# A two-layer graph network on one core: four more tiles' step 0 output made between the parts of step 1's first list, and the tail's tiles in another order

## Chip, cores and metric

One core of a Trainium2 chip runs the whole program in one launch. The metric is device time in microseconds (us), from the first to the last instruction and what lies around it. Lower is better. The engines are PE (matrix products and transposes; PEld is its weight load), ACT (pointwise functions and copies out of the accumulators), DVE (vector operations, maxima, sums), POOL (simple vector operations and indirect DMAs) and SP (which only issues DMAs). Each takes its instructions strictly in order.

## The reference, cut to what matters

`x` has 3327 rows of 256 numbers, `adj` is a sparse 0/1 matrix of 3327 x 3327. Layer 0 is a graph attention with a gated update, and its result, normalized by row, is `X` for layer 1:

```python
R = S + eye(N); R = R / R.sum(-1, keepdims=True)      # S is adj
Z = 0; Xf = X; Xa = X
for n in range(2):                                     # "step 0" and "step 1"
    A  = top_p_attention(Xa, W1, W2, W3)               # softmax, keep the largest to 0.9 of the sum
    Xf = R @ Xf
    Xa = A @ Xa
    Z  = Z + Xf @ U1[n].T + Xa @ U2[n].T
h = X + Z
out = layernorm(h) * ln_g + ln_b
x = layernorm(X + out)
```

The output of a row needs four products with 256 x 256 matrices: two of step 0 (`Xf @ U1[0].T`, `Xa @ U2[0].T`) and two of step 1.

## The kernel before

Rows are cut into 26 tiles of 128 (the last has 127). Step 0 of layer 1 handles one tile every 32 turns of a hand-written order. Step 1 handles the tiles one after another in a pipelined loop: while PE transposes and multiplies the attention of tile i (`product`), DVE sorts the logits of tile i+1 (`list_1`, `list_2`, `list_3`) and masks them (`mask`), and ACT takes exponentials (`exp`, `exp_list`). Rows whose list was too short are put aside, and up to three tiles of them ("hard" tiles) are worked off in the tail.

Three stages matter here.

**The gap between step 0 and step 1.** Tile 0 of step 1 has no product before it, so its list is made alone: `list_1(NT)`, two `exp`, `list_2`, `exp_list`, `list_3`, `mask`, `put_aside_1`, and only then the loop with `propagate` (a product with the adjacency) and `product`. The order of PE, ACT and DVE in this block is the order of the text (`manual_schedule`). POOL and SP are placed by the framework's scheduler, which also hands out the buffers.

**The early ends.** For the first `HALVES` = 10 tiles the two step 0 products are made during the last tiles of step 0 (`early_ends`). A tile's five parts are `transposes` (four transposes of its rows `xfe` and of `xa`), `copy` (ACT, accumulator to `xt`), `load_next` (the load of the tile two further on), `terms` (eight matmuls and the addition of `X` as a product with the identity, into `pze`) and `store` (ACT copies `pze` to `z`, SP writes it to `z0_rows` in DRAM). The rows `xfe` come from DRAM into a buffer of the tag `xf`, of which there are two. The loop's own rows (`xf`, made by `fetch`) have the same tag, and the tiles `z` share the tag `own`, also of two, with a tile that `propagate` fills on POOL.

**The tail.** `ends` works off the hard tiles on DVE (`bound`, `hard`), each followed by a product on PE (`hard_end`), and opens one `tile_end` after another between them: 0.8 for each turn. A tile end loads its rows, transposes them, multiplies, and normalizes twice over ACT, DVE and POOL. In this text an F tile is one whose end makes both steps (16 of them: two loads of rows and one of `X`, eight transposes, 16 matmul instructions plus two for `X`) and an H tile one whose step 0 part is read back from `z0_rows` (10 of them: half the transposes and half the matmuls). The order before is all F tiles (10 to 25), then all H tiles (0 to 9).

Of the kernel before, what the change touches and what calls it, by code (L numbers as in the profile page):

```python
# [9 lines left out]
F32 = mybir.dt.float32  # L10
# [6 lines left out]
P = 128  # L17
N = 3327
D = 256
DC = D // P  # L20
DA = 64
NT = (N + P - 1) // P
# [65 lines left out]
]  # L88
AT_0 = {name: tick for tick, name in ORDER_0}

HALVES = 10

GROUP = (208, 167)
LIST = (40, 72)
# [14 lines left out]
def rows(t):  # L109
    return TAIL if t == NT - 1 else P  # L110
# [13 lines left out]
def move_rows(engine, dst, src, r):  # L124

    full = r // 16 * 16
    for a, b in ((0, full), (full, r)):
        if a < b:
            engine.dma_start(dst[a:b], src[a:b])
# [170 lines left out]
class SlowLayer1:  # L300
# [33 lines left out]
    def transposed(self, srcs, r, tag):  # L334

        nc = self.nc
        xt = self.work.tile([P, 2 * DC, P], F32, tag="xt", name=f"xt{tag}")
        pt = self.psm.tile([P, 2 * DC, P], F32, tag="sm", name=f"ptx{tag}")
        for s, a in enumerate(srcs):
            for c in range(DC):  # L340
                nc.tensor.transpose(pt[:, s * DC + c, :r], a[:, c * P : (c + 1) * P], self.ident[:r, :r])
        m = len(srcs) * DC
        nc.scalar.copy(xt[:, :m, :r], pt[:, :m, :r])
        return xt
# [827 lines left out]
class Layer1:  # L1172
# [52 lines left out]
    def setup_0(self, keep, dram):  # L1225

        nc, sh = self.nc, self.sh


        self.fromend = keep.tile([P, 1], F32, name="fromend")  # L1230
        nc.vector.tensor_scalar(self.fromend, sh.rowid[:, 0:1], -1.0, float(P), ALU.mult, ALU.add)
        self.block = keep.tile([P, NT], BF16, name="block")
        nc.vector.tensor_scalar(self.block, sh.col1[:, :NT], -1.0, float(NT), ALU.mult, ALU.add)

        self.places_l = keep.tile([P, UL], BF16, name="places_l")
        nc.vector.tensor_scalar(self.places_l, sh.col1[:, :UL], -1.0, None, ALU.add)
        self.places_h = keep.tile([P, UH], BF16, name="places_h")
        nc.vector.tensor_scalar(self.places_h, sh.col1[:, :UH], -129.0, None, ALU.add)
        self.zeros = keep.tile([P, NT], F32, name="zeros26")
        nc.vector.memset(self.zeros, 0.0)  # L1240

        self.needed = keep.tile([P, NT], F32, name="needed")
        self.ulist = dram.tile([NT, UB * P], F32, name="ulist")

        self.z0_rows = dram.tile([HALVES * P, D], F32, name="z0_rows")

    def sparse(self, t):

# [350 lines left out]
    def early_ends(self):  # L1599


        nc, sh = self.nc, self.sh
        while self.phase <= EVERY0 * (NT - 1) + AT_0["logits3"]:
            yield
        self.load_u1()
        xfs, xts, pzs = {}, {}, {}

        def load(t):
            xfs[t] = self.work.tile([P, D], F32, tag="xf", name=f"xfe{t}")
            move_rows(nc.sync, xfs[t][: rows(t)], sh.xf_rows[t * P : t * P + rows(t), :], rows(t))  # L1610

        def load_next(t):
            if t + 2 < HALVES:
                load(t + 2)

        def transposes(t):
            turn = self.transposing((xfs.pop(t)[: rows(t)], self.xa[: rows(t), t, :]), rows(t), f"et{t}")
            next(turn)
            xts[t] = turn

        def copy(t):
            xts[t] = next(xts[t])

        def terms(t):
            pzs[t] = self.pac.tile([P, 512], F32, tag="av", name=f"pze{t}")
            self.output_terms(pzs[t], xts.pop(t), 0, (0, 1), rows(t), True, False)
            self.plus(pzs[t], sh.x1[: rows(t), t, :], rows(t))

        def store(t):
            z = self.work.tile([P, D], F32, tag="own", name=f"z0_{t}")  # L1630
            nc.scalar.copy(z[: rows(t)], pzs.pop(t)[: rows(t), :D])
            move_rows(nc.sync, self.z0_rows[t * P : t * P + rows(t), :], z[: rows(t)], rows(t))

        load(0)
        load(1)
        at = {}
        for i, turns in enumerate(((2, 3, 4, 24, 28), (17, 18, 19, 25, 29))):
            at.update(zip(turns, [(i, f) for f in (transposes, load_next, copy, terms, store)]))
        while self.phase % EVERY0 != 5:
            yield  # L1640
        for t in range(0, HALVES, 2):
            for k in range(EVERY0):
                if k in at:
                    i, f = at[k]
                    f(t + i)
                yield

    def first_1(self):


        while self.phase <= EVERY0 * (NT - 1) + max(AT_0[k] for k in ("sign0", "sign1", "xf")):
            yield
        v = self.item(NT)
        self.item(NT + 1)
        self.fetch(NT)
        v.cand = self.candidates(v.r, GROUP[1], v.tag)
        ready, waiting = [], list(range(-(-N // GROUP[1])))
        for pair in self.chunks():
            while self.done * P < min(NT * P, HALF + pair[0][1] + LC):
                yield  # L1660
            for i in (NT, NT + 1):
                self.some_logits(i, pair)
                yield
            ready += [c for h, s in pair for c in range(h * HALF + s, min(N, h * HALF + s + LC))]
            have = set(ready)
            for g in list(waiting):
                if have.issuperset(range(g * GROUP[1], min(N, (g + 1) * GROUP[1]))):
                    waiting.remove(g)
                    self.eights(v.cand, v.l, v.r, GROUP[1], g * GROUP[1], min(N, (g + 1) * GROUP[1]))
            yield  # L1670

    def transposed(self, srcs, r, tag, kind="xt"):

# [284 lines left out]
    def tile_end(self, t, j):  # L1958

        nc, r, sh = self.nc, rows(t), self.sh  # L1960
        on = slice(t * P, t * P + r)
        a = self.work.tile([P, EB, P], F32, tag="m", name=f"xfs{t}").rearrange("p b c -> p (b c)")
        xa2 = self.work.tile([P, D], F32, tag="xf", name=f"xa2_{t}")
        x1 = self.work.tile([P, D], F32, tag="xf2", name=f"x1_{t}")[:r]

        spare = lambda k: sh.qT[:r, k * D : (k + 1) * D]
        h, xb = spare(j % 9), spare(9 + j % 3)
        steps = (0, 1) if t >= HALVES else (1,)
        if 0 in steps:
            move_rows(nc.sync, a[:r, :D], sh.xf_rows[on, :], r)  # L1970
        move_rows(nc.sync, a[:r, D : 2 * D], sh.xf2_rows[on, :], r)
        move_rows(nc.sync, xa2[:r], sh.xa2_rows[on, :], r)
        move_rows(nc.sync, x1, (sh.x1_rows if 0 in steps else self.z0_rows)[on, :], r)
        yield
        srcs = ((a[:r, :D], self.xa[:r, t, :]), (a[:r, D : 2 * D], xa2[:r]))
        xts = [self.transposed(srcs[n], r, f"{'uv'[n]}t{t}") for n in steps]
        yield
        pz = self.pac.tile([P, 512], F32, tag="av", name=f"pzt{t}")
        for n, xt in zip(steps, xts):
            self.output_terms(pz, xt, n, (0, 1), r, n == steps[0], False)  # L1980
        self.plus(pz, x1, r)
        yield
        rest = self.output_rows(pz, [xb], h, r, f"t{t}")
        for k, _ in enumerate(rest):
            if k == 2:
                move_rows(nc.sync, xb, sh.xb_rows[on, :], r)
            yield
        move_rows(nc.sync, self.out[on, :], h, r)
# [255 lines left out]
    def ends(self, bounds):  # L2244


        ends = [self.tile_end(t, j) for j, t in enumerate((*range(HALVES, NT), *range(HALVES)))]
        open_ends, queue = [], []
        ticks = 0

# [49 lines left out]
    def run(self):  # L2300
# [4 lines left out]
            self.step_0()  # L2305
        with self.tc.manual_schedule(engines=engines):
            self.list_1(NT)
            self.exp(NT, 0)
            self.exp(NT, 1)
            self.list_2(NT)  # L2310
            self.exp_list(NT)
            self.list_3(NT)
            self.mask(NT)
            self.put_aside_1(NT)
            for i in range(NT, total):
                if i + 2 < total:
# [141 lines left out]
```

## Time and profile before

| What | Value |
|---|---|
| time, three runs | 1824.83, 1835.53, 1836.32 us (median 1835.53) |
| the profiled execution's own time | 1836.04 us |
| its span, first to last instruction | 1834.2 us |
| mean granted PE clock | 0.927 |
| layer 0 and step 0 | to about 972 us |
| the gap (list of step 1's first tile, alone) | 972 to 988.8 us |
| step 1's loop | 988.8 to about 1577 us, 22.8 us per tile on average |
| the tail | about 1577 to 1834 us |
| last matmul, last store of a tile end | 1798.5 us, 1819.8 us |

The profiled execution agrees with the median of the runs to 0.5 us, so sums can be made against it. Times in the views are us from the start of the span. In a timeline each line gives start, busy time, engine, source line, operation, what it writes and reads, how many were merged, and in brackets the idle time before it and what ended that.

### The profile page before, as it was taken

The page shows a single profiled execution, that of the slowest core. Times are in us where ns is not written, and L with a number is a line of the kernel's source. Part 1 is how long each engine was busy: PE and PEld are TensorE (multiplying, and loading weights), DVE is VectorE, ACT ScalarE, POOL GpSimd, SP SyncE. Part 2 cuts the span into 40 slices and gives each one's busy share as a digit, 9 for nine tenths or more (in the row PEclk, how much of TensorE's full clock was granted, in tenths as well). Part 3 has the DMA queues.
Part 4 walks back from the last instruction along what each step waited for, and adds up shares of the span by engine and source line. Part 5 has one row for each costly group of instructions (what it writes and reads, how often), then busy time and mean ns, then how long its engine had stood idle before and what let it go on. Part 6 is the DMA issues. An engine that isn't in the chain of part 4 may idle for free. (4 is left out here: it accounts for less than half of the span.)

```text
span 1834.2 us, 28832 instructions
## 1 busy us (share of the span) xinstructions
PE 1566.7 (85%) x8445; PEld 1093.6 (60%) x8445; DVE 1398.3 (76%) x4759; ACT 1060.3 (58%) x2398; POOL 1076.7 (59%) x1774
## 2 busy tenths in 40 slices
PE   6489999976898888888788999999999989788972
PEld 4255555544555555555565777777777656577861
DVE  5788887447887887877617999999999877967761
ACT  3366666645667667767624555555555446567544
POOL 1577777634665565555444556666666573655754
PEclk9799999987989898989988999999999999899986
DMA  8877773322333333333331111111111120223231
GB/s 268 293 258 238 232 224 100 83 68 76 94 100 101 87 98 103 91 96 102 92 96 44 47 50 50 53 53 49 47 50 50 49 59 20 67 63 95 78 87 46
DMA packets 115301, 181.38 MB, mean 99 GB/s; under 512 B 27900, under 2 KB 84213, under 8 KB 115136
## 3 DMA queue, kind: packets, MB, share of 16 engines
q0 software_dynamic: 26624, 74.64, 15.6%
q1 hardware_dynamic: 70258, 87.96, 14.9%
q10 hardware_dynamic: 18254, 16.86, 2.8%
q8 instruction: 69, 1.13, 0.2%
q14 instruction: 96, 0.79, 0.1%
HBM read 146.08 MB, written 33.41 MB: 98 GB/s over the span
## 5 line engine op out<-in xcount | busy, mean ns | idle before, releaser
L1917 PE MATMUL pav<-xa,at 128*128 128x256 f32 (+2 forms) x1352 | 331.4, 390 | 7.0 <-ACT at L1903 7.0
L1917 PEld LDWEIGHTS pav<-xa,at 128*128 128x128 f32 (+2 forms) x1352 | 245.7, 191 | 86.7 <-ACT at L1903 38.9
L1716 DVE MAX8 cand<-array 128x8 f32<-128x167 f32 (+5 forms) x921 | 241.3, 336 | 31.4 <-ACT array L1703 23.0
L1703 ACT COPY array<-pl 128x416 f32<-128x416 f32 (+3 forms) x402 | 183.5, 509 | 127.5 <-PE pl L1700 112.4
L1700 PE MATMUL pl<-kT,qT 64*128 64x416 f32 (+3 forms) x804 | 228.4, 599 | 17.3 <-issue 5.6
L647 POOL DMA_INDIRECT g<-xf_rows,edge x130 | 135.8, 1044 | 167.3 <-PE pxf L1860 126.0
L647 POOL DMA_INDIRECT g<-x_rows,edge x130 | 135.5, 1042 | 82.2 <-issue 32.9
L1903 ACT COPY at<-pt 128x512 f32<-128x512 f32 (+2 forms) x182 | 96.3, 542 | 140.7 <-PE pt L1901 95.2
L647 POOL DMA_INDIRECT g<-whx,edge x130 | 141.1, 1085 | 46.4 <-issue 36.1
L1493 POOL DMA_INDIRECT g<-x1k,uidx x130 | 137.4, 1057 | 40.0 <-issue 38.6
L1734 DVE MAX8 lst<-cand 128x8 f32<-128x160 f32 (+3 forms) x364 | 113.5, 312 | 8.1
L1700 PEld LDWEIGHTS pl<-kT,qT 64*128 64x128 f32 (+1 forms) x804 | 77.2, 197 | 68.0 <-issue 33.9
L864 DVE FIND_INDEX8 at<-ones,array 128x8 uint32<-128x840 f32 (+1 forms) x104 | 105.5, 1027 | 0.0
L1832 DVE MATCH_REPLACE8 array<-gone,array 128x3335 f32<-128x3335 f32 (+1 forms) x26 | 94.0, 3617 | 0.0
L1736 DVE MATCH_REPLACE8 cand<-lst,cand 128x160 f32<-128x160 f32 (+3 forms) x312 | 92.9, 298 | 0.0
L1852 POOL TENSOR_SCALAR m<-col,erow 128x128 f32<-128x128 f32 x130 | 76.7, 603 | 1.0
L1860 PE MATMUL pxf<-g,m 128*128 128x256 f32 (+1 forms) x260 | 68.3, 413 | 3.4 <-DVE base L2023 3.4
L985 PE MATMUL acc<-g,m 128*128 128x259 f32 (+1 forms) x260 | 64.8, 397 | 6.8 <-ACT m L981 6.8
L1860 PEld LDWEIGHTS pxf<-g,m 128*128 128x128 f32 (+1 forms) x260 | 50.6, 203 | 31.0 <-issue 20.2
L1488 POOL TENSOR_SCALAR uidx<-back 128x5 uint32<-128x5 f32 x26 | 9.8, 378 | 97.9 <-DMA back<-ulist 97.8
L1554 PE MATMUL pav<-g,w 128*128 128x257 f32 (+1 forms) x260 | 63.7, 389 | 1.2 <-issue 0.7
L1554 PEld LDWEIGHTS pav<-g,w 128*128 128x128 f32 (+1 forms) x260 | 47.1, 189 | 21.6 <-issue 7.0
(568 smaller groups left out, 3897.9 us busy)
## 6 DMA issues: line engine op xcount, KB each, us to landing
array<-in_adj_dram SPq DMA_DIRECT2D x23, 1248.0 KB
array<-in_adj_dram SPq DMA_DIRECT2D x23, 415.5 KB
xf_rows<-xf SPq DMA_DIRECT2D x50, 128.0 KB
xa_rows<-xa SPq DMA_DIRECT2D x50, 128.0 KB
xfs<-xf_rows SPq DMA_DIRECT2D x40, 128.0 KB
whx<-table ACTq DMA_DIRECT2D x25, 129.5 KB
x_rows<-x ACTq DMA_DIRECT2D x25, 128.0 KB
x1k<-x ACTq DMA_DIRECT2D x25, 128.0 KB
```

Source lines behind the costliest of these rows:

```text
L647: self.nc.gpsimd.indirect_dma_start(out=dst[:, b, :], out_offset=None, in_=table[:, :], in_offset=bass.IndirectOffsetOnAxis(ap=self.edge[: ...
L864: nc.vector.max_index(at[:r, g, :], self.ones8[:r], ad[:r, g, :])
L1493: nc.gpsimd.indirect_dma_start(out=v.g2[:, b, :], out_offset=None, in_=sh.x1k[:, :], in_offset=bass.IndirectOffsetOnAxis(ap=v.idx[:, b : b ...
L1554: nc.tensor.matmul(v.acc[:r, : D + 1], v.w[:, b, :r], v.g2[:, b, : D + 1], start=(b == 0), stop=(b == UB - 1))
L1700: nc.tensor.matmul(pl[:r, :w], q[on], self.sh.kT[on, n, s : s + w], start=True, stop=True)
L1703: nc.scalar.copy(l[:r, h * HALF + s : h * HALF + s + w], pl[:r, :w])
L1716: self.nc.vector.max(cand[:r, g * 8 : g * 8 + 8], src[:r, g * group : min(N, (g + 1) * group)])
L1734: nc.vector.max(lst[:r, k : k + 8], cand[:r])
L1832: nc.vector.match_replace(rev, gone[:r], rev, -BIG)
L1860: nc.tensor.matmul(acc[:r, :D], v.m[:, b, :r], v.g[:, b, :], start=(b == 0), stop=(b == EB - 1))
L1903: nc.scalar.copy(at[:, :full, :r], pt[:, :full, :r])
L1917: nc.tensor.matmul(v.acc[: v.r, :D], at[:k, j - 4 * g, : v.r], V[:k, j, :], start=(j == 0), stop=(j == NT - 1))
```

## The change

`MORE` = 4 further tiles (10 to 13) get the treatment of the first ten. Their parts are not run in step 0. They are kept in a list of ten entries, each for two tiles, and `some_ends(n)` runs the next n entries. Two entries come after `list_1(NT)`, four after `list_2(NT)`, three after `list_3(NT)` and one after `mask(NT)`. In the tail there are now 14 H tiles and 12 F tiles, and they are sorted so that both kinds are spread evenly: F14, H0, H1, F15, H2, F16, H3, F17, H4, F18, H5, F19, H6, F20, H7, H8, F21, H9, F22, H10, F23, H11, F24, H12, F25, H13.

```diff
-HALVES = 10
+HALVES, MORE = 10, 4
...
-        self.z0_rows = dram.tile([HALVES * P, D], F32, name="z0_rows")
+        self.z0_rows = dram.tile([(HALVES + MORE) * P, D], F32, name="z0_rows")
...
         def load_next(t):
-            if t + 2 < HALVES:
+            if t + 2 < HALVES + MORE:
                 load(t + 2)
...
+        self.more_ends = []
+        for t in range(HALVES, HALVES + MORE, 2):
+            both = (t, t + 1)
+            self.more_ends += [[lambda f=f, i=i: f(i) for i in both] for f in (transposes, copy, load_next, terms, store)]
...
+    def some_ends(self, n):
+
+        for _ in range(n):
+            for f in self.more_ends.pop(0):
+                f()
...
-        steps = (0, 1) if t >= HALVES else (1,)
+        steps = (0, 1) if t >= HALVES + MORE else (1,)
...
-        ends = [self.tile_end(t, j) for j, t in enumerate((*range(HALVES, NT), *range(HALVES)))]
+
+        less = HALVES + MORE
+        order = sorted(range(NT), key=lambda t: (t + 0.5) / less if t < less else (t - less + 0.3) / (NT - less))
+        ends = [self.tile_end(t, j) for j, t in enumerate(order)]
...
             self.list_1(NT)
+            self.some_ends(2)
             self.exp(NT, 0)
             self.exp(NT, 1)
             self.list_2(NT)
+            self.some_ends(4)
             self.exp_list(NT)
             self.list_3(NT)
+            self.some_ends(3)
             self.mask(NT)
+            self.some_ends(1)
             self.put_aside_1(NT)
```

So the new order of PE in the gap is transposes of 10 and 11, terms of 10 and 11, transposes of 12 and 13, terms of 12 and 13, and then, as before, the flag's product, `propagate` and `product`. On ACT it is copies of 10 and 11, both exponentials, stores of 10 and 11, the list's exponential, copies of 12 and 13, stores of 12 and 13. DVE gets no new instruction.

## The prediction

> **What bounds the kernel now.** I read the page first, then the windows, then the timelines of the two stages that the change touches, engine by engine, then the waits of SP's queue.
>
> ```profile
> span 1834.2 us, 28832 instructions
> PE 1566.7 (85%) x8445; PEld 1093.6 (60%) x8445; DVE 1398.3 (76%) x4759; ACT 1060.3 (58%) x2398; POOL 1076.7 (59%) x1774
> ```
>
> PE looks like the bound, but the mean hides the two stages. The windows of the gap (length, then busy time and count of PE, PEld, DVE, ACT, POOL, then the granted clock) show PE and ACT with room and DVE without:
>
> ```profile
> 970.00:975.00 5.00, 5.00 (x22) 3.19 (x21) 4.36 (x20) 3.87 (x7) 0.00 (x0) 1.00 0.08 26
> 975.00:980.00 5.00, 2.09 (x10) 1.60 (x9) 4.21 (x19) 2.77 (x7) 1.17 (x2) 1.00 0.15 52
> 980.00:985.00 5.00, 2.85 (x8) 2.31 (x8) 4.80 (x8) 0.00 (x0) 2.93 (x10) 0.61 0.15 37
> 985.00:990.00 5.00, 2.93 (x11) 2.06 (x10) 4.91 (x9) 0.49 (x2) 2.90 (x2) 0.50 0.04 15
> 990.00:995.00 5.00, 5.00 (x16) 3.76 (x14) 4.93 (x23) 1.15 (x2) 3.92 (x5) 0.52 0.37 107
> ```
>
> The timeline of the same stretch says who waits for whom:
>
> ```profile
> 972.58 0.34 SPq L129 DMA_DIRECT2D xf<-xf_rows  x1
> 973.35 1.68 ACT L1784 ACTIVATE array<-array,pay 128x1664 f32<-128x1664 f32 x1
> 978.76 0.35 ACT L1797 ACTIVATE e<-lst,pay 128x71 f32<-128x71 f32 x1 [1.26 <-DVE e L1796]
> 982.15 0.16 PE L2001 MATMUL pos<-flag,lower 128*128 128x1 bf16 x1 [5.06 <-POOL flag L1999]
> 988.85 1.94 PE L1901 MATMUL pt<-ident,array 128*128 128x128 f32 x8 [2.07 <-DVE array L1818]
> 990.62 3.78 PE L1917 MATMUL pav<-xa,at 128*128 128x256 f32 x8
> 1003.13 0.31 DVE L1804 TENSOR_TENSOR_SCAN before<-e 128x72 f32<-128x72 f32 x1 [2.56 <-ACT e L1797]
> 1014.20 1.99 PE L1917 MATMUL pav<-xa,at 128*128 128x256 f32 x8 [0.29 <-ACT at L1903]
> ```
>
> The end of the gap is the mask at 988.70, which is DVE's chain. `exp_list` at 978.76 stands in it and everything behind `exp_list` follows without idle time. ACT had done both exponentials at 976.78, 2 us before they were needed. After the gap PE works at half clock (0.52): eight `pav` matmuls take 3.78 us against 1.99 later, and DVE then waits 2.56 us for an exponential behind those late copies. From mask to mask the first tile of the loop takes 24.0 us (988.70 to 1012.69), the second 21.8. The loop hands on any delay of its start one to one, since both PE and DVE are nearly full in it.
>
> In the tail DVE has the long chain, and it stalls where a tile end or a hard tile's product on PE is late:
>
> ```profile
> 1641.20 0.43 DVE L1880 BATCH_NORM_STATS2 bnat<-qT 128x6 f32<-128x256 f32 x1 [7.34 <-ACT qT L1941]
> 1664.28 0.43 DVE L1880 BATCH_NORM_STATS2 bnah<-xh 128x6 f32<-128x256 f32 x1 [5.16 <-ACT xh L1941]
> 1734.61 0.43 DVE L1880 BATCH_NORM_STATS2 bnah<-xh 128x6 f32<-128x256 f32 x1 [4.40 <-ACT xh L1941]
> 1768.24 1.97 PE L1901 MATMUL pth<-ident,array 128*128 128x128 f32 x8 [5.87 <-DVE array L2179]
> ```
>
> **The change, the gap.** One tile's four transposes take 0.44 us on PE in a row of work (1737.30 to 1737.74), its terms 2.16 (972.61 to 974.77). On ACT a copy costs 0.59 and a store 0.37. Four tiles make 10.4 us of PE and 3.8 of ACT, against 5.06 + 2.07 us of idle PE and 7.72 us of idle ACT in the gap. It is not the sum that decides but the order and the loads. SP's waits show it (total, times, longest):
>
> ```profile
> SPq L129 <- PE ptxet L1684: 31.6, 8, 14.0
> ```
>
> Each `xfe` load waits for the transposes of the tile before, because one of the two `xf` buffers is held from 912.4 on by the loop's first tile. The load of tile 10 takes the place of the `xf` load at 972.58. No `xfe` load has its own wait, so I price it by a store of the same size: issued 977.07, POOL goes on at 978.83, so 1.76 us. Working it out:
> 1. Load 10 lands at 974.3. PE reaches it after the last terms of tile 9 at 977.1, transposes done 977.5.
> 2. Load 11 is issued only then, lands at 979.4, transposes done 979.9, copy 11 on ACT done 980.5.
> 3. Both exponentials stand behind copy 11 on ACT: 980.5 + 3.43 (973.35 to 976.78) = 984.0, where DVE's list is ready at 978.7.
> 4. Terms 10 and 11 end at 979.9 + 2 x 2.16 = 984.2, so the stores end at 984.8, `exp_list` at 985.1, and `list_3` starts at 985.2 instead of 979.14: **6.1 us late**. Queued behind it are mask, the first product and the loop.
> 5. Tiles 12 and 13: loads 12 and 13 again one after the other (982 and 986.9), terms at 987.3 to 991.7, flag and `propagate` 2.4, so 994.2. The mask ends at 988.70 + 6.1 = 994.8. PE is covered by 0.6 us; if it runs at half clock it is some 2 us late.
> 6. PE is now busy up to the product. If the clock stays up, the first cycle takes 21.8 instead of 24.0: **2.2 us back**.
>
> Gap: 6.1 - 2.2 = **+3.9 us**. Low end: the scheduler puts transposes 10 before terms 9, which takes 1.7 off step 2, and the clock is fully warm: +2. High end: terms 10 and 11 at half clock (the row 3.78 against 1.99 makes that +2), no time back, PE 2 late in step 5: +10. The added DMAs are four loads that come early (paid in steps 1, 2, 5) and four stores of 128 KB that nothing here waits for except through buffers.
>
> What clock do terms 10 and 11 get after PE's new idle time of 1.9 us before transposes 11? At 1729.2 PE idles 1.57 us and then 0.46, and the next four matmuls take 1.69 us against 1.13 warm, so I count such a gap as cold in the high end. The Trainium skill ("TensorE: Matmul & The Clock Gate", Part 1: The HAM clock gate) says that the clock falls after about 3.4 us of idle time, which speaks for warm terms here; by it the gap costs +3.9 as in the sum, by the row up to +5.9.
>
> **The change, the tail.** An F tile's end takes 0.88 + 3.88 = 4.76 us of PE (1696.54 to 1697.42 and 1709.32 to 1713.20), an H tile's 0.44 + 2.16 = 2.60 (1737.30 and 1737.74 to 1739.90). Each of the four that turn saves 2.16 us of PE, one ACT copy (0.5 in a row of copies) and one load. Since ticks are unchanged, the n-th place in the order keeps its time. Counting `pzt` groups on PE:
> - Places 0 to 4 (1586 to 1623): were five F, now F H H F H. DVE runs its own chain here; the coarse sums on ACT end about 1 us earlier, which takes away DVE's 0.97 us wait at 1618.87: **-1.0**.
> - Places 5 to 7 (inside the first hard product, 1636 to 1660): F H F. PE runs without gaps to the 5.16 us stall: **-2.2**.
> - Places 8 to 13: three H of six; stalls of 2.17 and 0.85 us behind ACT, of which half: **-1.5**.
> - Places 14, 15 (second hard product): two H where two F were. 2 x 2.16 = 4.3, under the stall of 4.40: **-4.3**.
> - Places 16 to 22: four F, three H, all H before. DVE's chain covers PE (3.6 and 5.87 us idle there); the like stretch with six F stalled 3.0 against 1.8 here: **+0.5**, up to +4 if loads are late.
> - Places 23 to 25 (last hard product, 1768 to 1798, PE full, DVE idle): H F H. 2.16 on the path to the end: **+2.2**.
>
> Tail: **-6.3 us**. Low end -11 (the whole of the two stalls of hard products and the waits of 1 us), high end +2 (late loads in the F places, no gain in places 8 to 13, half of the rest).
>
> **Sum.** 1836.0 + 3.9 - 6.3 = 1833.6, call it **1834 us**: no change that can be told. This forecast's own range is 1827 to 1848 by the ends.
>
> **Rivals.**
> *A, the tail is worth more.* The hard products start when PE is free (1623.3 and 1701.3) and not when their rows are ready (1617.0 and 1698.3). If lighter places let them start then, all three stalls go: 7.34 + 5.16 + 4.40 = 16.9, with the gap at +2: 1836 - 16.9 + 2 = 1821 us. For it: PE is continuously busy from 1598 to 1623. Against it: ACT copies the first hard product's transposes only at 1627.6, behind its coarse sums, whatever PE does.
>
> *B, slower: POOL holds up the gap.* `z` and `propagate`'s POOL tile share two buffers of the tag `own`. If POOL's queue has that tile's instruction, waiting for the store of `z` 13, ahead of the flag's instructions, then PE's flag product, `propagate` and the first product wait too. Store 13 would end on ACT at about 992.5, land at 994.3, the flag follows 3.4 us later (978.83 to 982.2), `propagate` cold 4.6: the product starts at 1002.9 instead of 988.85, +14.1 with no time back, and the tail gives -4: 1846 us. For it: in the trace that instruction (979.12) does stand between two of the flag's. It decides as soon as it is queued before the flag. Against it: the scheduler may put it last.
>
> *C, slower: F tiles late in the tail.* The stretch 1742.8 to 1747 has 84.5% of the DMA engines' time on SP's queue, and PE waited up to 3.58 us there for rows, with H tiles only. Four F bring four more loads. At 3.6 each that is +14.4, with the last F +2.2, against -9 from the earlier places and +3.9 in the gap: 1848 us. Against it: DVE's chain hides PE in most of it.
>
> **Chances.** Forecast 0.52, A 0.16, B 0.19, C 0.13. About what a measurement of this kernel can tell from no change is 1%, 18 us. A lies near that border with a lucky run (the runs before spread from 1824.8 to 1836.3): 0.11 of it and 0.03 of the forecast pass. Of B and C, if they add up or the gap is at its high end, 0.16, and 0.05 of the forecast. So faster 0.14, same 0.65, slower 0.21. The range goes from A's side, 1818, to a little beyond C, 1852.
>
> **What would show it.** The gap: `exp_list` at about 985 behind two stores, the mask's end near 994.8, PE idle some 2 us before transposes 11, the granted clock of the next 5 us near 1.0 and the first cycle near 21.8. The tail: stalls at `xh` of about 3 and 0 us instead of 5.16 and 4.40, the last `pavh` group 2 us later after its hard mask. Wrong would be: the exponentials still at 976 (copies not in the way), POOL's `own` before the flag (B), PE waiting for `xfs` rows in places 16 to 22 (C), or a DVE that does not stall at all between 1634 and 1664 (A).

## The result, and the profile after

The changed kernel takes 1833.59 us (median of 18 runs, 1829.89 to 1839.51) against 1835.71 us before (18 runs, 1824.83 to 1839.95). The ratio is 0.9995 with a 95% interval of 0.9982 to 1.0008: no change that can be told. The profiled execution took 1834.0 us.

The head of the page after (span; then busy time, share of the span and instructions of each engine):

```profile
span 1832.2 us, 28862 instructions
PE 1560.8 (85%) x8453; PEld 1092.3 (60%) x8453; DVE 1398.9 (76%) x4759; ACT 1062.3 (58%) x2402; POOL 1083.4 (59%) x1774
```

PE has 5.9 us less work and no other engine has moved by more than 7 us. As before, the stages tell more than the mean. The windows of the gap (length, busy time and count of PE, PEld, DVE, ACT, POOL, then granted clock, DMA share, GB/s):

```profile
970.00:975.00 5.00, 5.00 (x14) 3.29 (x14) 4.64 (x21) 1.60 (x3) 0.00 (x0) 0.50 0.09 26
...
980.00:985.00 5.00, 4.24 (x15) 3.57 (x16) 0.00 (x0) 3.57 (x4) 0.00 (x0) 0.71 0.20 67
...
990.00:995.00 5.00, 5.00 (x27) 4.37 (x26) 4.91 (x4) 1.13 (x3) 1.50 (x8) 1.00 0.19 56
```

Before, DVE was busy for 4.2 to 4.9 us of each such window; now it stands still from 977 to 988. The clock is at half speed at the beginning (0.50), where it was at 1.00 before, and it dips again at 980 to 985. The timeline of the same stretch shows for what DVE waits:

```profile
980.76 0.41 PE L1695 MATMUL ptxet<-ident,xfe 128*128 128x128 f32 x2 [2.01 <-DMA xfe<-xf_rows]
981.43 0.59 ACT L1698 COPY xtet<-ptxet 128x512 f32<-128x512 f32 x1 [2.05 <-PE ptxet L1695]
981.91 1.68 ACT L1795 ACTIVATE array<-array,pay 128x1664 f32<-128x1664 f32 x1
982.10 1.90 PE L1944 MATMUL pze<-u,xtet 128*128 128x256 f32 x4
...
987.48 0.37 ACT L1631 COPY z<-pze 128x256 f32<-128x256 f32 x1 [1.87 <-issue]
987.75 0.36 ACT L1808 ACTIVATE e<-lst,pay 128x71 f32<-128x71 f32 x1
988.14 0.31 DVE L1815 TENSOR_TENSOR_SCAN before<-e 128x72 f32<-128x72 f32 x1 [10.79 <-ACT e L1808]
...
994.99 3.53 POOL L1876 TENSOR_SCALAR own<-xf,rinv 128x256 f32<-128x256 f32 x1 [3.03 <-DMA z_rows<-z]
...
999.09 1.99 PE L1928 MATMUL pav<-xa,at 128*128 128x256 f32 x8 [0.24 <-ACT at L1914]
```

The order is that of the prediction: load 11 only after the transposes of tile 10, the exponential at 981.91 directly behind copy 11, the list's exponential (987.75) directly behind the second store. It is 2.7 us later than the forecast's 985.1: the transposes of tile 11 end 1.3 us later than its 979.9, and the terms of tiles 10 and 11 take 6.0 us instead of 4.3, four of them 1.90 us instead of 1.03 (982.10). The first eight `pav` matmuls are warm (1.99 against 3.78 before).

The tail, on DVE:

```profile
1644.87 0.43 DVE L1891 BATCH_NORM_STATS2 bnat<-qT 128x6 f32<-128x256 f32 x1 [5.14 <-ACT qT L1952]
1667.95 0.43 DVE L1891 BATCH_NORM_STATS2 bnah<-xh 128x6 f32<-128x256 f32 x1 [4.47 <-ACT xh L1952]
1732.32 0.42 DVE L1891 BATCH_NORM_STATS2 bnah<-xh 128x6 f32<-128x256 f32 x1
```

The stall of 7.34 us has become 5.14, that of 5.16 has become 4.47, and the one of 4.40 is gone.

### The profile page after: what moved, and what is told of

It is laid out like the page before. It is cut to its first block, busy times and chain, and to the rows that moved or that the text cites. A ratio compares the mean times of both kernels' runs of the same rounds, so it can differ in the third digit from the quotient of the medians.

```text
span 1832.2 us, 28862 instructions
## 1 busy us (share of the span) xinstructions
PE 1560.8 (85%) x8453; PEld 1092.3 (60%) x8453; DVE 1398.9 (76%) x4759; ACT 1062.3 (58%) x2402; POOL 1083.4 (59%) x1774
## 5 line engine op out<-in xcount | busy, mean ns | idle before, releaser
L1727 DVE MAX8 cand<-array 128x8 f32<-128x167 f32 (+5 forms) x921 | 241.3, 335 | 29.2 <-ACT array L1714 17.8
L647 POOL DMA_INDIRECT g<-whx,edge x130 | 141.2, 1086 | 46.5 <-issue 36.1
L1711 PEld LDWEIGHTS pl<-kT,qT 64*128 64x128 f32 (+1 forms) x804 | 78.6, 200 | 68.7 <-issue 36.3
```

The costliest lines, as they stand in the source:

```text
L647: self.nc.gpsimd.indirect_dma_start(out=dst[:, b, :], out_offset=None, in_=table[:, :], in_offset=bass.IndirectOffsetOnAxis(ap=self.edge[: ...
L1711: nc.tensor.matmul(pl[:r, :w], q[on], self.sh.kT[on, n, s : s + w], start=True, stop=True)
L1727: self.nc.vector.max(cand[:r, g * 8 : g * 8 + 8], src[:r, g * group : min(N, (g + 1) * group)])
```

## Measuring by stages

The total scatters by 10 us from run to run, so I compare stages. They lie between points that every trace has on DVE: the end of the last reciprocal of step 0 (at 966.08 us before and 964.35 after), those behind the first, the second and the last mask, those of the three hard tiles, and the starts of the hard tiles' statistics `bnah`. A "product" below is the stretch from a hard tile's reciprocal to its `bnah`. `pl` is the busy time of the eight `pl` matmuls in the last logits that step 0 makes, just ahead of the gap: 3.5 us at full clock, 4.4 to 4.6 where the clock falls in them.

| kernel | pl | to first mask | first cycle | loop | to hard 0 | product 1 | to hard 1 | product 2 | to hard 2 | product 3 | to the end | sum |
|---|---|---|---|---|---|---|---|---|---|---|---|---|
| before | 3.48 | 23.02 | 23.98 | 546.5 | 57.8 | 46.9 | 34.5 | 35.8 | 34.0 | 28.3 | 37.3 | 868.1 |
| before_again | 4.35 | 24.61 | 22.77 | 549.1 | 57.7 | 45.2 | 34.5 | 34.5 | 33.4 | 28.4 | 37.0 | 867.2 |
| after | 4.60 | 33.91 | 22.01 | 545.2 | 57.8 | 44.7 | 34.4 | 30.0 | 32.6 | 31.0 | 36.2 | 867.9 |
| after_again | 3.47 | 29.14 | 22.03 | 544.6 | 57.7 | 44.7 | 34.4 | 29.9 | 32.7 | 31.0 | 36.2 | 862.4 |
| parts_only | 3.47 | 30.91 | 22.02 | 545.0 | 57.7 | 46.9 | 34.9 | 30.1 | 34.0 | 28.6 | 36.1 | 866.2 |
| order_only | 3.47 | 23.02 | 24.08 | 544.7 | 57.7 | 44.7 | 33.7 | 33.2 | 33.7 | 30.9 | 37.2 | 863.1 |
| exp_first | 3.47 | 23.01 | 26.99 | 545.3 | 57.8 | 44.9 | 34.4 | 29.9 | 32.7 | 31.1 | 36.2 | 862.3 |
| free_loads | 4.43 | 30.34 | 23.12 | 544.5 | 57.8 | 44.6 | 34.4 | 30.0 | 32.6 | 31.0 | 36.5 | 864.9 |
| placed | 3.47 | 29.12 | 22.44 | 543.5 | 57.8 | 41.3 | 34.5 | 30.2 | 33.2 | 28.5 | 36.4 | 856.8 |
| light_first | 3.47 | 29.21 | 22.00 | 544.8 | 57.8 | 41.1 | 34.3 | 33.6 | 32.6 | 37.1 | 36.9 | 869.3 |
| all_mended | 4.48 | 24.61 | 24.93 | 544.9 | 57.7 | 41.3 | 34.5 | 30.2 | 33.2 | 28.5 | 36.3 | 856.1 |
| ten_placed | 3.47 | 23.03 | 23.79 | 544.6 | 57.7 | 41.2 | 34.5 | 30.8 | 32.7 | 29.2 | 37.1 | 854.6 |

The experiments ran on three other chips, where all kernels, the one before too, take about 40 us less; nearly all of that lies ahead of the table (step 0 ends at 925 to 933 us instead of 964 to 966). Within the table a stage that an edit doesn't touch repeats to a few tenths, except where the clock falls. Ratios are to the kernel before on the same chip.

From before to after the table reads: gap +8.9 (10.9 in the first stretch, 2.0 back in the first cycle), loop -1.3, tail -7.9, together -0.3; a further 1.7 us of the 2.0 between the spans lies ahead of the gap, in code that the change does not touch.

## The experiments

Theory: the gap costs 4 us or more, through ACT's order and the loads one after the other; the tail gives 6 to 8, and only where a light (H) tile takes the place of a full (F) one inside a hard product. Rivals: the gains come from the work saved, wherever it lies; only one of the two causes in the gap counts.

**Once more before and after.**

> The kernel before once more, for its stages on this chip: from step 0's last reciprocal 23.0 and 24.0 us in the gap, 274.6 us of tail; the stretch of the loop between (546.5 in the first profile) 544.5 to 548 with the clock in its last five tiles.

> The changed kernel once more, for its stages on this chip. Theory (the gap's length depends on whether the clock falls during the last logits of step 0, after pauses of 1.05 and 0.46 us): first mask 33.9 us after the last reciprocal if the eight pl matmuls take 4.4 to 4.6 us, 29 to 31 if they take 3.5; tail 266.7 us within 0.5 either way.

Measured (one execution of each): the gap of `after_again` is 29.14 + 22.03 = 51.2 us instead of 55.9, with all of its terms at full clock. Against before (47.0) that is +4.2. The instructions up to the last logits are the same in all fourteen traces, pauses of 1.05 and 0.46 us on PE among them; in six of them the clock falls in the `pl` matmuls, in eight it does not. The lines of `after_again` that answer to those of the gap:

```profile
944.76 0.41 PE L1695 MATMUL ptxet<-ident,xfe 128*128 128x128 f32 x2 [1.91 <-DMA xfe<-xf_rows]
950.45 0.31 DVE L1815 TENSOR_TENSOR_SCAN before<-e 128x72 f32<-128x72 f32 x1 [6.39 <-ACT e L1808]
960.07 1.09 PE L1912 MATMUL pt<-ident,array 128*128 128x128 f32 x8 [0.60 <-DVE array L1829]
```

Step 0's last reciprocal is at 931.41 here, so `list_3` starts 19.04 us after it, against 13.06 before: 6.0 us late. DVE waits 6.39 us instead of 10.79.

`before_again` shows that the kernel before has such luck too: 270.8 us of tail instead of 274.6. In its first hard product the clock did not fall, and 1.7 of the 3.9 us lie there, 1.3 in the second. `warm_gap` and `warm_short` below have the tail of before, the fall too, and 274.2 and 273.9 us. The window 10 us behind hard 0's reciprocal, first of before, then of `before_again` (the granted clock is third from the end, 0.73 and 1.00):

```profile
1627.36:1632.36 5.00, 4.14 (x15) 3.52 (x16) 4.04 (x8) 1.89 (x5) 4.67 (x5) 0.73 0.17 52
```

```profile
1594.35:1599.35 5.00, 4.16 (x22) 3.65 (x23) 4.04 (x8) 1.87 (x5) 4.67 (x5) 1.00 0.16 52
```

Its `pl` were slow, which cost 1.6 us to the first mask and came back in part: PE then had less idle time ahead of the flag's product (3.69 instead of 5.06 us). So the tail gives 4.2 to 7.9 us by which of the two runs one compares with; the expected 274.6 was wrong for this one, and its loop of 549.1 us lies outside the expected 544.5 to 548.

**One half of the change at a time.**

```diff
 # parts_only: the changed kernel with
-        order = sorted(range(NT), key=...)
+        order = (*range(less, NT), *range(less))
 # order_only: the kernel before with
+        less = HALVES
+        order = sorted(range(NT), key=...)
```

> The change without its new order in the tail: fourteen step 0 parts made early, four of them between the parts of step 1's first list, and in the tail first the twelve full tiles, then the fourteen light ones, as the order was written before. By the prediction's terms the gap is that of the changed kernel: list_3 starts about 988 us (before 979.1), the first mask ends about 997.7, and after the first cycles the loop is 5 to 6 us behind. The tail: places 12 to 15 turn from full to light; two of them, 14 and 15, lie in the second hard product, which gets 4.3 us shorter (5.9 by what the changed kernel shows); places 12 and 13 lie under DVE's chain and give nothing; the first and last hard products keep their lengths of before. Sum -0.5 to +2 us against before. Rival: the gains of the tail come from the interleaving alone; then the second product keeps its stall of 4.4 us on DVE and the kernel is 5 to 6 us slower than before.

> Only the order in the tail is changed: ten light tiles as before, spread evenly among the sixteen full ones; nothing is added to the gap. Gap: list_3 at 979.1, the first mask at 988.7, as before. The order is F H F F H | F H F | F H F H F F | H F | F H F H F F H | F H F (bars: before the first hard product, in it, between, in the second, between, in the last). By places at 2.16 us for a light tile on PE inside a product: first product one light tile, -2.2; second product one light, -2.2 to -3; last product two full tiles, +4.3 to +5.4; the stretches between cost and gain nothing. Sum 0 to -0.5 us, same. Rival (what turns a full tile into a light one counts wherever it is): the work of the tail is the same, so nothing changes in any stretch by more than 1 us. Second rival: five full tiles late in the tail wait for their rows, +3.6 us each in places 16 to 25: +10 us or more.

Measured: `parts_only` 1797.26 us against 1795.82, ratio 0.9999 (0.998 to 1.0019); `order_only` 1795.28, ratio 0.9985 (0.9965 to 1.0005). By the total neither can be told from before. By stages both theories hold in the main and their rivals fall (the tails are compared with `before`, in whose first product the clock falls as it does in these two): `parts_only` pays 5.9 us in the gap and gets 5.7 back in the second product, where places 14 and 15 have turned light; its other stretches of the tail are those of before within 0.4 us, but for 1.2 us at the end. Its sum is 1.0 and 1.9 us below those of the two traces of before, where -0.5 to +2 was expected; its loop is shorter by 1.5 and more. `order_only` has the gap of before, gains 2.2 and 2.6 in the first and second product, where it has one light tile each, and loses 2.6 in the third. I had expected 4.3 to 5.4 there, for full tiles at 23 and 25: PE begins the terms of the tile at place 25 only after the third product, so 23 and 24 alone count. Its stretch after the second product (33.7) shows no late rows.

**The two causes in the gap.**

```diff
 # exp_first: the changed kernel with
             self.list_1(NT)
-            self.some_ends(2)
             self.exp(NT, 0)
             self.exp(NT, 1)
             self.list_2(NT)
-            self.some_ends(4)
             self.exp_list(NT)
+            self.some_ends(6)
 # free_loads: the changed kernel with, for t >= HALVES,
-            xfs[t] = self.work.tile([P, D], F32, tag="xf", ...)
+            xfs[t] = self.work.tile([P, 4, D], F32, tag="hx", ...)[:, 0, :]
```

> The changed kernel with the two exponentials, list_2 and exp_list of step 1's first tile issued ahead of the first six parts of the four tiles (transposes, copies, loads, terms, stores), so that ACT doesn't hold the list behind copies and stores. Theory 1 (ACT's order alone sets the gap): exp_list at about 978, list_3 at 978 instead of 988.1, the mask ends at about 988, the product starts there, some 8 us gained against the changed kernel. Theory 2 (PE's chain of four loads, one after the other, sets it as soon as ACT doesn't): list_3 and the mask come early (978, 988), but PE reaches the first product's transposes only when terms 12 and 13 and the propagation are done, at 994 to 997; the first scores of the product start 1 to 3 us earlier than in the changed kernel (997.8), and 1 to 3 us are gained in all.

> The changed kernel with the four added tiles' rows loaded into two buffers that are idle at that time (those of the hard tiles' rows), so that a load no longer waits for the transposes of the tile before. Theory 2 (the loads one after the other set the gap): the wait of 2.0 us before transposes 11 goes, copies and exponentials come 3 to 4 us earlier, the terms of tiles 10 and 11 run without a pause ahead of them, list_3 starts at 983 to 985 instead of 988.1, the mask ends at 993 to 994 instead of 997.7: 4 to 5 us gained against the changed kernel. Theory 1 (ACT's order): the exponentials stand behind copies 10 and 11 still; they are only 1 to 2 us earlier, and so is the mask.

Measured: `exp_first` 1795.36 us, ratio 0.999 (0.9971 to 1.001); `free_loads` 1795.39, ratio 0.9995 (0.9977 to 1.0013). In `exp_first` the list and the mask are on time again, and it helps little:

```profile
942.40 0.31 DVE L1815 TENSOR_TENSOR_SCAN before<-e 128x72 f32<-128x72 f32 x1 [0.41 <-ACT e L1808]
...
951.88 0.08 DVE L1829 DVE_READ_ACCUMULATOR array<-array,t,array 128x1 f32 x1
...
957.45 1.04 PE L1912 MATMUL pt<-ident,array 128*128 128x128 f32 x8
```

The mask is ready at 951.96, but PE comes to the product only at 957.45, with no idle time before it: two waits for rows of 2.20 and 2.02 us and four tiles' work stand in between. Gap 50.0 us against 51.2, so 1.2 us gained (theory 2). In `free_loads` the waits on PE are gone and the mask is now the later one:

```profile
945.34 0.31 DVE L1815 TENSOR_TENSOR_SCAN before<-e 128x72 f32<-128x72 f32 x1 [7.58 <-ACT e L1808]
...
954.96 1.09 PE L1912 MATMUL pt<-ident,array 128*128 128x128 f32 x8 [2.27 <-DVE array L1829]
956.29 3.60 PE L1928 MATMUL pav<-xa,at 128*128 128x256 f32 x8 [0.24 <-ACT at L1914]
```

Its `pl` were slow, so I count from the transposes of tile 10: to `list_3` it is 6.6 us (938.74 to 945.34) against 8.2 in `after_again` (942.26 to 950.45). That is 1.6 us and not the 4 to 5 that I expected of theory 2; it is what theory 1 said. The two causes stand one behind the other: whichever is taken away, the other holds the product. The idle 2.27 us then also cost warm matmuls (3.60).

**What the first cycle's length is.**

```diff
 # the kernel before with, between list_3 and mask (24 in warm_gap, 11 in warm_short)
+            pd = self.psm.tile([P, 512], F32, tag="sm", name="warm")
+            for k in range(24):
+                nc.tensor.matmul(pd[:, :D], self.ident, sh.x1[:, 0, :], start=(k == 0), stop=(k == 23))
```

> The kernel before with 24 matmuls of 128x256 more on PE between list_3 and the mask of step 1's first tile, into a tile that nobody reads: nothing else is changed. Theory (the time back in the first cycle is the clock's): PE is busy where it was idle for 5.1 us, the product after the mask runs at a granted clock near 1.0 instead of 0.5, its first eight pav matmuls take 2.0 instead of 3.8 us, the first cycle 21.8 to 22.2 instead of 24.0, and step 0's last reciprocal to the second one of step 1 45.0 to 45.4 instead of 47.0 to 47.1. Rival (the first cycle is longer for its late copies and exponentials, whatever the clock): 24.0 stays.

> The kernel before with 11 matmuls of 128x256 more on PE between list_3 and the mask (24 made 10.5 us and held PE past the mask; 11 make 4.8 us), into a tile that nobody reads. Theory (the clock's): PE is free again before the flag is there, propagation takes 2.4 instead of 4.6 us, the mask ends as before (23.0 us after step 0's last reciprocal, 24.6 if the clock falls in the last logits), the first eight pav matmuls take 2.0 us and the first cycle 21.8 to 22.2 instead of 24.0 us. Rival (late copies and exponentials): 24.0 stays.

Measured: neither settles it by itself. In `warm_gap` (1794.18 us, ratio 0.9999, 0.998 to 1.0018) each matmul became two instructions, 10.5 us in all; the product ran at full clock from its start, as expected, but PE came to it 2.0 us after the mask's reciprocal, and first mask and cycle took 24.61 + 23.74. In `warm_short` (1793.39 us, one run) the added work took 4.9 us, PE was done before the mask, stood idle once more, and the clock fell again:

```profile
949.09 1.63 PE L1901 MATMUL pt<-ident,array 128*128 128x128 f32 x8 [3.20 <-DVE array L1818]
950.54 3.12 PE L1917 MATMUL pav<-xa,at 128*128 128x256 f32 x8
```

Its cycle of 22.76 is that of `before_again` (22.77), with slow `pl` in both and as good as the same `pav`, so the added matmuls did nothing and the expectation failed. What the traces together show is how the time from the product's first transposes to the second mask goes with the first eight `pav`:

| first eight pav, us | product's start to second mask, us | traces |
|---|---|---|
| 1.99 | 21.7 to 22.5 | after, after_again, parts_only, light_first, placed, exp_first, all_mended, warm_gap |
| 3.12 to 3.22 | 23.0 | warm_short, before_again |
| 3.60 | 23.45 | free_loads |
| 3.78 | 24.0 to 24.3 | before, order_only, ten_placed |

By this table the clock at the product's start is worth some 2 us, as the prediction had it: the order holds in kernels whose copies and exponentials lie differently. It is an order among kernels and not an experiment, since an edit that changes the clock alone was not achieved.

**What a place is worth.**

```diff
 # placed and all_mended: the changed kernel with
-        order = sorted(range(NT), key=...)
+        light = (5, 6, 7, 14, 15, 16, 17, 18, 19, 21, 22, 23, 24, 25)
+        kinds = [iter(range(less, NT)), iter(range(less))]
+        order = [next(kinds[k in light]) for k in range(NT)]
 # all_mended: and both edits of exp_first and free_loads
 # light_first: the changed kernel with
+        order = (*range(less), *range(less, NT))
 # ten_placed: the kernel before with light = (5, 6, 7, 14, 15, 21, 22, 23, 24, 25)
```

> The changed kernel with the fourteen light tiles not spread evenly but put where PE is on the path: at places 5, 6, 7 (first hard product), 14 to 19 and 21 to 25 (second and last product); full tiles at 0 to 4, 8 to 13 and 20. Theory (a light tile is worth 2.2 to 2.9 us of PE inside a hard product and nothing elsewhere): against the changed kernel the stretch up to the first product's statistics falls from 44.7 to 40.4 us, that of the second stays at 30.0, the last falls from 31.0 to 28.4, the stretches between grow by 1.3 us at most; the tail from the last mask on falls from 266.7 to about 261. Rival (the first product's end is set by ACT's copies and not by PE, as the stall of 4.5 us behind ACT suggests): 44.7 stays above 43, and only the last product gains, about 3 us in all.

> The changed kernel with all fourteen light tiles first in the tail, then the twelve full ones: the gap and the work are the same, only places differ. Theory (worth by place): first product's stretch 40.4 us as in the kernel placed, second 35.8 (two full tiles, as before), last 28.3 + 3 x 2.2 to 2.9 = 35 to 37, the stretch between the second and the last with full tiles only 34 to 38; tail 272 to 278 us against 266.7 of the changed kernel and 274.6 of the kernel before: with the gap's 6 to 9 us the kernel is slower than the kernel before by 4 to 12 us. Rival (the work alone counts: four light tiles more save 8.6 us of PE wherever they lie): the tail stays within 2 us of 266.7.

> The changed kernel with three edits: exponentials, list_2 and exp_list ahead of the first six parts; the four added loads in buffers that are idle then; the light tiles at the places of the kernel placed. Theory: the stretches add up. Gap: first mask 23.0 us after step 0's last reciprocal (changed kernel 30.9 to 33.9), first cycle about 23 us since PE is ready 24 to 25 us after that reciprocal instead of 28; so 46 to 47 us for both against 47.0 before and 55.9 in the changed kernel. Tail 261 us against 266.7. From step 0's end to the end 851 to 854 us, 9 to 15 us below the kernel before: ratio 0.992 to 0.995. Rival (what is gained in the gap is given back in the loop or the tail because tiles or loads stand ready later): 860 us or more, ratio above 0.997.

> The kernel before with its own ten light tiles put at places 5, 6, 7, 14, 15 and 21 to 25 of the tail, full tiles elsewhere; no part is added to the gap. Theory (a light tile counts only at the places inside the three hard products, and ten places suffice): the gap as before (47.0 us from step 0's last reciprocal to the second mask's), first product's stretch 41.3 us, second 30.2, last 28.5, as in the kernel placed; tail 261 to 264 us against 274.6 before; from step 0's end to the end 854 to 857 us, as far below the kernel before (868 and 863 in the runs so far) as the kernel with all three mends and four tiles more; ratio 0.993 to 0.996. Rival (the fourteen are needed because full tiles at 16 to 19 wait for their rows): the stretch after the second product grows from 33.2 by 3 us or more, ratio 0.997 or above.

Measured:

| kernel | us | before, same chip | ratio, 95% interval |
|---|---|---|---|
| placed | 1788.81 | 1793.48 | 0.9971 (0.9958 to 0.9985) |
| light_first | 1797.58 | 1793.48 | 1.0022 (1.0004 to 1.0041) |
| all_mended | 1783.54 | 1793.48 | 0.9945 (0.9925 to 0.9965) |
| ten_placed | 1784.38 | 1794.48 | 0.9950 (0.9933 to 0.9966) |

The same fourteen light tiles with the same work make the kernel 0.3% faster or 0.2% slower by their places alone, so "only the work counts" falls. The first product takes 46.9, 44.7 and 41.2 us with none, one and three light tiles (places 5 to 7), 1.9 us for a tile; in all of these the clock falls in it, and without the fall none takes 45.2 (`before_again`). The third takes 28.3 to 29.2 with none full at 23 and 24, 30.9 to 31.1 with one, some 2.5 for a tile, and 37.1 in `light_first`, where PE is so far behind that the full tile of place 22 lies in it as well. In `light_first` the second product took 33.6 us against an expected 35.8, and the stretch behind it 32.6 against 34 to 38. `placed` came out at 261.8 us of tail against the expected 261, and `all_mended` at 261.7 with a gap of 49.5. I had expected 46 to 47 there; the `pl` fell to half clock, transposes 10 started 13.8 us after step 0's last reciprocal instead of 10.85, and without these 3 us it would be 46.6 (an estimate).

`ten_placed` is the lesson of the study: ten light tiles, none of the change's additions to the gap, and as much gained as by all three mends to the changed kernel. Its first two products on DVE:

```profile
1619.40 0.43 DVE L1880 BATCH_NORM_STATS2 bnah<-xh 128x6 f32<-128x256 f32 x1 [3.35 <-ACT xh L1941]
1684.70 0.43 DVE L1880 BATCH_NORM_STATS2 bnah<-xh 128x6 f32<-128x256 f32 x1 [0.52 <-ACT xh L1941]
```

Where DVE stalled for 5.16 and 4.40 us before, it stalls for 3.35 and 0.52. Both versions beat the kernel before and, at 0.9945 and 0.9950 against 0.9995, the changed one. Between the two the intervals decide nothing.

## Why the prediction was right, point by point

The forecast of 1834 us was met (1833.59), and the cause is the forecast's: a loss in the gap against a gain in the tail. That it was met to 0.4 us is luck, and the table shows it: in the profiled pair the gap cost 5.0 us more than forecast and the tail gave 1.6 more, and 1.3 us in the loop and 1.7 ahead of the gap came from stretches for which the sum had nothing. Where the clock stayed up in the gap (`after_again`), the sum of the stages is 4.8 and 5.7 us below the two traces of before, against a forecast of 2.4. In the gap the mechanism is the forecast's, and a size was off. In the tail the sum came out near, but two of its terms had the mechanism wrong (places 0 to 4 and 8 to 13).

| term of the sum | forecast | after against before | remark |
|---|---|---|---|
| `list_3` late (steps 1 to 4) | +6.1 | +10.7 | 6.0 in `after_again` at full clock |
| mask's end (step 5: 994.8) | 28.7 us after the reciprocal | 33.3 | 28.6 in `after_again` |
| first cycle (step 6) | -2.2 | -2.0 | right |
| gap | +3.9 | +8.9 | +4.2 in `after_again` |
| loop | 0 | -1.3 | the clock falls in one and not in the other, see below |
| places 0 to 4 | -1.0 | 0.0 | wrong: DVE's wait is still 0.97 |
| places 5 to 7 | -2.2 | -2.2 | right, but in another stall |
| places 8 to 13 | -1.5 | -0.1 | comes out in the next row |
| places 14, 15 | -4.3 | -5.9 | with the row above -6.0 against -5.8 |
| places 16 to 22 | +0.5 | -1.3 | wrong sign, small |
| places 23 to 25 | +2.2 | +2.7 | right |
| end of the tail | not priced | -1.1 | open |
| tail | -6.3 | -7.9 | |

*The gap.* The chain of steps was right to 0.3 us in the run in which the clock stayed up. In the profiled run after it fell twice. It fell in the last logits and the terms of tile 8, ahead of the gap: that moved transposes 10 by 2.9 us (13.8 instead of 10.85 us after the reciprocal), and the prediction had no term for it. And it fell after the pause for load 11: terms 10 and 11 took 6.0 us (981.23 to 987.24) instead of 4.3, which the prediction had as its high end of +2. So the term that was off is the duration of the matmuls. It was taken from one execution; it should have been given both ends and the odds.

*Rule and row.* The Trainium skill ("TensorE: Matmul & The Clock Gate", Part 1: The HAM clock gate) puts the fall after an idle window of some 3.4 us, and also calls that window free-running, so that the same kernel differs from run to run. The second half agrees with the runs, in so far as the same instructions do not always meet the same clock. In `after`, `parts_only` and `placed` one group of terms behind a pause of about 2 us ran at half clock; in `after_again`, `exp_first` and `light_first` all stayed warm behind the same pauses. The first half, read as a threshold on one pause, is not borne out: in 6 of 14 traces the clock fell in the `pl` matmuls with no longer pauses than 1.05 and 0.46 us in the 25 us ahead of them. That these pauses are the cause is not shown: the same pair stands 13.4 and 26.9 us earlier too, and there the clock stayed up in all fourteen.

*Places 0 to 4.* The forecast was that ACT's coarse sums would end earlier and take away DVE's wait of 0.97 us at 1618.87. They did end earlier, 3.7 us ahead of the reciprocal instead of 0.7, and DVE waited 0.97 us all the same (at 1624.74). Behind the sums POOL adds two columns; before, then after:

```profile
1616.76 0.26 POOL L2111 TENSOR_TENSOR bothh_0.5_18394<-sums4h_0.5_18354 128x2 f32<-128x2 f32 x1 [10.03 <-ACT array L2105]
```

```profile
1619.59 3.29 POOL L2122 TENSOR_TENSOR bothh_0.5_18441<-sums4h_0.5_18402 128x2 f32<-128x2 f32 x1 [7.45 <-ACT array L2116]
```

After, the addition starts inside a DVE instruction over the whole rows (1619.18 to 1622.83, `x<-x,th`) and ends with it; before, it starts 0.2 us from that instruction's end. So it ends 0.35 us ahead of the reciprocal in both, whenever the sums are ready. In `light_first` it starts 0.1 us ahead of that instruction and takes 0.20 us, and DVE's wait falls to 0.68.

The first hard product starts 10.86 us after the reciprocal in both kernels, since it waits for this chain (timeline after, around that product's start):

```profile
1625.07 4.07 POOL L1895 TENSOR_TENSOR mvat<-mvat,power 128x1 f32<-128x1 f32 x1
1629.17 0.29 ACT L1902 ACTIVATE shiftat<-shiftat,mvat 128x1 f32<-128x1 f32 x1 [6.76 <-POOL mvat L1895]
1633.48 1.05 ACT L1914 COPY ath<-pth 128x512 f32<-128x512 f32 x2
1634.09 3.64 PE L1928 MATMUL pavh<-xa,ath 128*128 128x256 f32 x8 [9.37 <-ACT ath L1914]
```

A tile's power (POOL's step of the normalization) ends at 1629.14, behind it ACT makes the coarse sums and only then copies the product's transposes. PE waits 9.37 us instead of 3.87. So the lighter places ahead of it only lengthened PE's idle time, and the product starts at half clock (3.64 us). The power itself takes 0.55 us alone (at 1635.20) and 4.07 under a DVE instruction of 3.69 us with two inputs (1625.00 to 1628.69). The Trainium skill ("SBUF — State Buffer", SBUF: two separate sides) says that DVE and GpSimd share a port pair, and that a DVE instruction with two SBUF inputs or a GpSimd instruction, whichever starts first, holds it for the whole instruction; these rows and those of the addition agree.

*Places 5 to 7.* The 2.2 us came out of the first stall (7.34 to 5.14) and not out of the stall at `xh`, which stayed at 4.47 where I had said 3. *Places 8 to 15.* The lighter places 8 to 13 don't shorten their own stretch, which is DVE's, but leave PE free for the second product. Timeline before, then after:

```profile
1701.30 1.04 PE L1901 MATMUL pth<-ident,x 128*128 128x128 f32 x8
```

```profile
1701.63 1.09 PE L1912 MATMUL pth<-ident,x 128*128 128x128 f32 x8 [0.46 <-DVE x L2190]
```

Before, PE came to it 2.5 us behind hard 1's reciprocal (1698.79), with no idle time; after, it waited for DVE and started 0.7 us ahead of the reciprocal (1702.37). That is 3.2 us, and two light tiles are 4.3 more. Of these 7.5 only 5.9 count: DVE reaches the statistics without a stall, so its own work is now the bound there. `light_first` tells the two apart: its PE comes to the second product as early as after, with two full tiles in it, and takes 33.6 us instead of 30.0, so two light tiles are worth 3.7 and the early start 0.9 to 2.2 (34.5 and 35.8 in the two traces of before).

*Places 16 to 22:* no F tile was late; PE waits for rows there fell to 0.95 us.

*The rivals.* A (tail worth 16.9) had its mechanism right for the second product, which now starts when its rows are ready, but not for the first, whose start did not move; and in `placed`, the order with the shortest tail, the tail is 12.8 us shorter than before. B did not come: POOL's `own` stands behind the flag, at 994.99 (B's terms add to 1002.3 and not to its 1002.9). C did not come: no stretch with F tiles late in the tail outside a product is longer than before. `light_first` shows what C's side of the sign would have been, by places and not by rows: 8.8 us in the third product.

*The loop's -1.3* is not shown to be the change's. The loop ran 543.5 to 549.1 us in all kernels, with its differences in the last five tiles, where PE pauses. In the last tile but one PE pauses for 2.04 us in all fourteen traces, behind the same instructions. Then the clock falls to half for 3.4 or 6.8 us in four of them, and the last tile takes 28.4 to 30.0 us; in the ten others it stays up, and the last tile takes 26.8. The four (`before`, `before_again`, `warm_gap`, `warm_short`) are those with the tail's order of before; whether that is chance is open.

Open: why the stretch after the third product is 0.6 to 1.2 us shorter with fourteen light tiles than with ten (but for `light_first`, 36.9 us), and what decides whether the clock falls in the last logits.

## What to carry to other kernels

Price work that is taken out of a queue by where it lies: here 2 to 3 us a tile inside a product that the longest chain waits for, and elsewhere nothing, unless PE comes to such a product earlier by it; then reorder what is there before making more of it. When work is put into a gap, follow both chains through it, since taking one wait away only hands the bound to the other. And where a total scatters by 10 us, cut the traces at points that both kernels have: stages repeat to tenths, and show gains and losses that the total hides.

## What the runs showed of the hardware that I had not expected

The granted clock is not fixed by the instructions: in fourteen traces with the same instructions up to there, eight `pl` matmuls took 3.5 us eight times and 4.4 to 4.6 us six times. One such fall cost the kernel before almost nothing (gap 47.0 and 47.4 us) and the changed one some 3 us, because the change had put work of PE on the gap's path. Four matmuls of 128x256 take 1.03 us at full clock and 1.90 at half.
